# Loading most of x in 32-column strips for VectorE to transpose, and regrouping one expert's rows later, in a routed feed-forward kernel

## The chip, the core and the metric

The kernel runs on one core of one Trainium2 chip. The metric is the device time of one execution in microseconds (us), the median of the runs. The core has five engines with one instruction stream each: TensorE (PE in the profile; PEld is its weight load), VectorE (DVE), ScalarE (ACT), GpSimd (POOL) and SyncE (SP), which here only starts DMAs. Each stream runs in order, so an instruction that waits holds up everything behind it on its engine.

## The reference

x has 4 batches of 1024 tokens of 512 floats. Each batch picks one weight matrix and one bias by its category; a router then sends each token to one of 8 experts, each of which takes at most 512 tokens (4096/8) in token order, and each expert is a two-layer network.

```python
xc   = einsum('bsd,bdh->bsh', x, W[cat]) + b[cat]      # per batch, 512 x 512
p    = softmax(xc @ Wr); e = argmax(p); p_tok = p[e]    # 8 experts
slot = rank of the token among those of its expert      # kept if below 512
h    = relu(xc[dispatch] @ W1[e])                       # 512 -> 2048
y    = (h @ W2[e]) * p_tok                              # 2048 -> 512
out  = x;  out[token] += y                              # for the kept tokens
```

## The kernel before, in words

**Matrix products.** All large products are done by a seven-product scheme (Strassen's, in Winograd's form): operands are cut into quadrants, VectorE makes sums and differences of quadrants (`sums`, `differences`, L163 to L173), TensorE makes seven products k = 1 to 7 in place of eight, and the results are gathered in three accumulators in PSUM called x, y and z (the table `BANK`). VectorE and ScalarE take intermediate states of these accumulators out (the *evictions*), so the next product of the same accumulator waits for them.

**The linear stage** handles x in eight chunks of 512 tokens, chunks 2b and 2b+1 being batch b. `load_x` (L249 to L258) brings a chunk of 1 MB into one of three buffers (the pool `xin`), one token to a row of 2 KB. `transpose_x` is called four times for a chunk; each call turns 128 tokens with four TensorE transposes into PSUM (L276), and ScalarE copies the result to `xT` (L277). After the fourth call VectorE makes the four sums (L293 to L296). `linear` (L491) makes the seven products, `finish` evicts them (L505, L532, L536) and stores the result to two DRAM tensors `xc_dram` (L514). `transpose_w`, `through`, `router`, `choose` and `rank` compute the routing beside it; `rank` scatters each token's number to its slot in DRAM (L463). The tables `beside` and `loads` say behind which product each of these calls stands: TensorE's and SyncE's orders are written out by hand. On VectorE, ScalarE and GpSimd a planner chooses the order, with hints: `soon` puts a step early, `behind` and `issue_after` put it after a named instruction.

**The expert stage** runs e = 0 to 7. `gather` (L704, GpSimd) fetches an expert's rows from `xc_dram`, four gathers for each half of the columns; `fetch(e)` issues those of expert e+1 and then the residual rows of e while expert e's first layer runs. Expert 0's rows are transposed on TensorE (L768). The rows of every later expert are first *regrouped*: `regroup(e, a)` has ScalarE copy pieces of 32 partitions so that the 32 x 32 blocks stand where their transposes belong (L747, 16 copies for an expert, from four calls), and then `turn(e)` has VectorE transpose the blocks (L754, four instructions). `first_layer(e, g, k)` (L787) makes product k of column group g (g = 0 to 3); it snapshots accumulator x after k = 1, 6 and 7 with ScalarE (L802), adds on VectorE (L806) and applies relu on ScalarE (L807, L814). After k = 3 VectorE makes the group's sums (L163 to L166). `second_layer(e, k)` (L848) multiplies all four groups, the last group's quarter last; `inner_product` (L901) makes the remaining products by a second level of the scheme. `between` starts the weight loads and, for expert 0, copies x to the output by DRAM-to-DRAM transfers in three pieces.

In the last group of an expert's first layer the four `regroup(e + 1, ...)` calls stand after products 2, 6, 5 and 7, so ScalarE copies the next expert's rows between its snapshots and relus.

Of the kernel before, what the change touches and what calls it, by code (L numbers as in the profile page):

```python
# [8 lines left out]
F32 = mybir.dt.float32  # L9
# [7 lines left out]
P = 128  # L17
# [5 lines left out]
def kernel(  # L23
# [11 lines left out]
    nc = tc.nc  # L35
    B, S, D = x.shape
    NCAT = cond_w.shape[0]
    E, _, F = w1.shape
    T = B * S
    CAP = -(-T // E)  # L40
    KC = D // P
# [3 lines left out]
    CT = XT * P  # L45
    HT = CT // 2
    SC = CAP // P
    HK = KC // 2
# [3 lines left out]
    NG = F // (2 * HB * P)  # L52
    W1G = 3
    NS = E * SC
    V = 32
    VB = P // V
    Q = 32
    ROW = 2
    xf = x.rearrange("b s d -> (b s) d")
# [38 lines left out]
    ident = const.tile([P, P], F32, name="ident")  # L98
# [78 lines left out]
    def load_w1(e, g):  # L177

        t = w1p.tile([P, 7, HK, HB * P], F32, tag="w1", name=f"w1_{e}_{g}")
        for half in range(2):  # L180
            f = half * F // 2 + g * HB * P
            nc.sync.dma_start(
                out=t[:, 2 * half : 2 * half + 2, :, :].rearrange("p a k f -> p (a k) f"),
                in_=w1[e, :, f : f + HB * P].rearrange("(k p) f -> p k f", p=P),
            )
        w1s[e, g] = t
# [5 lines left out]
    with (  # L192
# [11 lines left out]
        cond, xrows, xT, xS, wT, logits, routed = {}, {}, {}, {}, {}, {}, {}  # L204
# [42 lines left out]

        def load_x(c, eng=nc.sync):
            t = xin.tile([P, XT, D], F32, tag="x", name=f"x_{c}")  # L249
            n = 1 if c == 0 else XT  # L250
            for j in range(0, XT, n):
                eng.dma_start(
                    out=t[:, j : j + n, :],
                    in_=xf[c * CT + j * P : c * CT + (j + n) * P, :].rearrange(
                        "(j p) d -> p j d", p=P
                    ),
                )
            xrows[c] = t  # L258

        def behind_this(f):  # L260
            with tc.issue_after(latest[0].ins):
                latest[0] = f()
# [5 lines left out]
        def transpose_x(b, i):  # L268


            c, j = b * 2 + i // XT, i % XT
            if j == 0:
                xT[c] = xtp.tile([P, KC, CT], F32, tag="xT", name=f"xT_{c}")
            ps = ps_t.tile([P, KC, P], F32, tag="t", name=f"ps_xT_{c}_{j}")
            for kc in range(KC):
                nc.tensor.transpose(ps[:, kc, :], xrows[c][:, j, kc * P : (kc + 1) * P], ident)  # L276
            nc.scalar.copy(xT[c][:, :, j * P : (j + 1) * P], ps)  # L277
            if j == XT - 1:
                a11, a12, a21, a22 = (
                    xT[c][:, k * HK : (k + 1) * HK, half * HT : (half + 1) * HT]  # L280
                    for half in range(2)
                    for k in range(2)
                )
                t = xsp.tile([P, 4, HK, HT], F32, tag="xs", name=f"xs_{c}")
                s1, s2, s3, s4 = (t[:, k, :, :] for k in range(4))
                if c == 2 * LATE + 1:

                    late["all"] = xin.tile([P, XT, D], F32, tag="x", name="late")
                if b == LATE:
                    s4 = lambda g: late["all"][:, 2 + g, :].rearrange("p (k n) -> p k n", n=HT)  # L290
                tt = nc.vector.tensor_tensor
                todo = [
                    lambda: tt(s1, a21, a22, ALU.add),  # L293
                    lambda: tt(s2, s1, a11, ALU.subtract),
                    lambda: tt(s3, a11, a21, ALU.subtract),
                    lambda: tt(s4, a12, s2, ALU.subtract),  # L296
                ]
                if c == 0:

                    b11, b12, b21, b22, t1, t2, t3, t4 = later_sums.pop(0)  # L300
                    todo[1:1] = [lambda: tt(t1, b12, b11, ALU.subtract)]
                    todo[3:3] = [lambda: tt(t2, b22, t1, ALU.subtract)]
                    todo[5:5] = [lambda: tt(t3, b22, b12, ALU.subtract)]
                    todo[7:7] = [lambda: tt(t4, b21, t2, ALU.subtract)]
                    rest = todo[4:]
                    latest[0] = todo[0]()
                    for f in todo[1:4]:
                        behind_this(f)
                    later_sums["rest"] = rest
                else:  # L310
                    if b == LATE:
                        late[c % 2] = (a12, s2)
                        todo[3:] = [
                            lambda g=g: tt(s4(g), *late[g], ALU.subtract)
                            for g in range(2)
                            if c % 2 == 1
                        ]
                    for f in todo:
                        f()
                    if late and b == LATE and c % 2 == 1:  # L320
                        for g in range(2):
                            xS.setdefault((LATE, g), s4(g))
                xS[c] = {1: a11, 2: a12, 3: s4, 4: a22, 5: s1, 6: s2, 7: s3}
# [300 lines left out]
        with tc.manual_schedule(engines={mybir.EngineType.PE, mybir.EngineType.SP}):  # L624
# [3 lines left out]
                out=wr_sb[:, :, 0:E], in_=wr.rearrange("(kc p) e -> p kc e", p=P)  # L628
# [16 lines left out]
            out=table.rearrange("p c e r -> p (c e r)"),  # L645
            in_=slots.rearrange("(p s) r -> p (s r)", p=P),
# [20 lines left out]
    rows, residual, xes, hs = {}, {}, {}, {}  # L667
# [68 lines left out]
    def regroup(e, a):  # L736


        if (e, "strips") not in rows:
            rows[e, "strips"] = xep.tile(  # L740
                [P, KC, SC, VB, V], F32, tag="strips", name=f"strips_{e}"
            )
        r = rows[e, "all"][a * V : (a + 1) * V].rearrange("p s (k b v) -> p s k b v", b=VB, v=V)
        for b in range(VB):
            into = rows[e, "strips"][b * V : (b + 1) * V, :, :, a, :]
            with tc.issue_after(snapped[0].ins):
                nc.scalar.copy(into.rearrange("p k s v -> p s k v"), r[:, :, :, b, :])  # L747
# [231 lines left out]
    with tc.manual_schedule(engines={mybir.EngineType.PE, mybir.EngineType.SP}):  # L979
        gather(0, xg, xc_dram, rows, src_row)  # L980

        for part, half, then in (
            (0, 0, [(0, 1)]),
            (0, 1, [(1, 1), (0, 5), (1, 5)]),
            (1, 0, [(0, 2)]),
            (1, 1, [(1, 2)]),
        ):
            for c in range(half * HC, (half + 1) * HC):
                transpose_rows(0, c, part)
            for g, k in then:  # L990
                first_layer(0, g, k)

        load_w2(0, xes[0][:, 3, 0, HC * P - 1 :])
        for e in range(E):
            for g in range(NG):
                if e == 0 and g < 2:

                    for k in ((6, 7), (4, 3))[g]:
                        first_layer(e, 0, k)
                        first_layer(e, 1, k)  # L1000
                    between(e, g)
                    continue
                first_layer(e, g, 1)
                first_layer(e, g, 2)
                if e + 1 < E and g == NG - 1:
                    regroup(e + 1, 0)
                between(e, g)
                for i, k in enumerate((6, 5, 7)):
                    first_layer(e, g, k)
                    if e + 1 < E and g == NG - 1:  # L1010
                        regroup(e + 1, i + 1)
            second_layer(e, 1)
            first_layer(e, NG - 1, 4)
            inner_sums(e, 2, sides="right")
            first_layer(e, NG - 1, 3)
            inner_sums(e, 2, sides="left")
            if (e + 1) * NG - 1 + W1G < E * NG:
                load_w1(e + 1, W1G - 1)

            def small(*turns):  # L1020
                for k, q in turns:
                    inner_product(e, k, q)

            second_layer(e, 6)
            inner_sums(e, 5)
            small(*[(2, q) for q in (1, 5, 2, 6, 3, 7)])
            second_layer(e, 7)
            small((2, 4))
            inner_sums(e, 3)
            inner_sums(e, 4)  # L1030
            if e + 1 < E:
                turn(e + 1)
            small((5, 5), (5, 2))
            if e + 1 < E:
                sum_xe(e + 1)
            small(
                *[(5, 1), (5, 3), (5, 6), (3, 5), (5, 7), (3, 2), (5, 4), (3, 1)],
                *[(4, 5), (4, 1), (3, 6), (4, 2), (4, 6)],
                *[(3, 3), (4, 3), (3, 7), (4, 7), (3, 4), (4, 4)],
            )  # L1040
            if e + 1 < E:
                load_w2(e + 1)
# [31 lines left out]
```

## Time and profile before

| what | value |
|---|---|
| median of 3 runs (range) | 941.21 us (940.35 to 941.21) |
| the profiled execution's own time | 936.94 us |
| its span, first to last instruction | 935.2 us |
| mean granted TensorE clock | 0.988 of full speed |
| busy share: PE, PEld, DVE, ACT, POOL | 97%, 86%, 71%, 28%, 19% |
| DMA packets, data | 95727, 123.31 MB |
| linear stage | start to about 147 us |
| expert 0 | about 147 to 268 us; experts 1 to 7 about 94 us each |

Times inside the execution are microseconds from the start of its span. In the row of slices each digit stands for a fortieth of the span (23.4 us) and is the busy share in tenths. Matmul durations in the groups overlap, since matmuls are pipelined; the pace of TensorE is read from the distance between starts.

### The profile page before, as it was taken

What the parts mean: (1) busy time and instruction counts of PE and PEld (TensorE: products, weight loads), DVE (VectorE), ACT (ScalarE), POOL (GpSimd) and SP (SyncE); (2) the same over time, 40 slices, a digit from 0 to 9 for tenths busy, and PEclk for the clock granted to TensorE, in tenths of its full rate; (3) what the DMA queues carried; (4) which work ended last, traced back from release to release, by engine and by line L of the source; (5) the groups of instructions that cost most, each with busy time, mean ns of one, the idle gap of its engine ahead of it and who ended that gap; (6) DMA issues with size and microseconds to landing.
All of it is one profiled execution on the core that took longest, in us unless ns stands there. A gap on an engine that the chain in (4) does not pass through costs nothing.

```text
span 935.2 us, 13219 instructions
## 1 busy us (share of the span) xinstructions
PE 902.6 (97%) x5204; PEld 807.9 (86%) x5204; DVE 660.5 (71%) x1226; ACT 264.9 (28%) x506; POOL 176.9 (19%) x173
## 2 busy tenths in 40 slices
PE   9999999928999999999999999999999999999996
PEld 6788787826998899889988998899889988998896
DVE  4656684625946995699569955995599559965893
ACT  3333201305023602360236013601360136013200
POOL 0042343060015001500150015001500140012001
PEclk9999999978999999999999999999999999999999
DMA  9474224991057205620462047214721363136001
GB/s 317 153 233 156 80 92 128 343 372 67 1 177 223 89 8 176 218 84 20 159 220 81 30 154 227 75 42 142 229 81 46 130 221 97 46 119 192 1 1 46
DMA packets 95727, 123.31 MB, mean 132 GB/s; under 512 B 8516, under 2 KB 83268, under 8 KB 95474
## 3 DMA queue, kind: packets, MB, share of 16 engines
q1 hardware_dynamic: 85058, 96.49, 31.3%
q0 software_dynamic: 9216, 24.85, 8.2%
q10 hardware_dynamic: 1392, 1.13, 0.4%
q8 instruction: 41, 0.67, 0.3%
q14 instruction: 20, 0.16, 0.1%
HBM read 105.96 MB, written 25.23 MB: 140 GB/s over the span
## 4 chain that ended last, share of the span: by engine, by line
PE 93%; DVE 2%; DMA 2%; POOL 1%; issue 1%; ACT 0%; POOLq 0%; DVEq 0%
PE hx L787 23%; PE yx L848 18%; PE yx L901 12%; PE hy L787 11%; PE yy L901 6%; PE xcx_lin L491 6%; PE hz L787 5%; PE yz L901 3%; PE xcy_lin L491 2%; PE ps_xT L276 2%; PE xcz_lin L491 1%; DMA rows_of<-xc_dram,at 1%; POOL rows_of L704 1%; PE ps_lT L382 1%; PE ps_wT L330 1%
## 5 line engine op out<-in xcount | busy, mean ns | idle before, releaser
L787 PE MATMUL hx<-xe,w 128*128 128x256 f32 x1024 | 239.6, 382 | 22.5 <-ACT s L802 21.4
L787 PEld LDWEIGHTS hx<-xe,w 128*128 128x128 f32 x1024 | 195.2, 192 | 49.4 <-ACT s L802 21.8
L946 POOL DMA_INDIRECT out_dram<-rows,dst_row x32 | 32.0, 999 | 477.0 <-DVE rows L833 416.4
L787 PE MATMUL hy<-xe,w 128*128 128x256 f32 x512 | 120.6, 379 | 0.0
L848 PE MATMUL yx<-w_b,h 128*128 128x256 f32 x512 | 113.4, 380 | 0.0
L787 PEld LDWEIGHTS hy<-xe,w 128*128 128x128 f32 x512 | 97.5, 190 | 13.0
L848 PEld LDWEIGHTS yx<-w_b,h 128*128 128x128 f32 x512 | 97.3, 191 | 12.8
L802 ACT COPY s<-hx 128x512 f32<-128x512 f32 x96 | 55.8, 581 | 173.0 <-PE hx L787 163.9
L806 DVE TENSOR_TENSOR h<-hy,s 128x512 f32<-128x512 f32 x64 | 44.2, 690 | 78.9 <-PE hy L787 51.6
L807 ACT ACTIVATE h<-h 128x512 f32<-128x512 f32 x96 | 60.5, 630 | 120.3 <-DVE h L806 120.1
L704 POOL DMA_INDIRECT rows_of<-xc_dram,at x56 | 63.1, 1127 | 140.7 <-DVE w L164 94.0
L901 PE MATMUL yx<-w_b,h 128*128 128x128 f32 x640 | 83.2, 275 | 0.0
L901 PEld LDWEIGHTS yx<-w_b,h 128*128 128x128 f32 x640 | 78.5, 192 | 0.8
L747 ACT COPY strips<-rows_of 32x512 f32<-32x512 f32 x112 | 69.0, 616 | 23.6 <-DMA rows<-in_x_dram,at 22.2
L787 PE MATMUL hz<-xe,w 128*128 128x256 f32 x256 | 60.6, 380 | 0.6 <-DVE xe L769 0.6
L806 DVE TENSOR_TENSOR h<-hz,s 128x512 f32<-128x512 f32 x32 | 22.0, 689 | 54.7 <-PE hz L787 54.7
L163 DVE TENSOR_TENSOR h<-h 128x512 f32<-128x512 f32 x64 | 43.7, 683 | 22.1 <-ACT h L807 22.1
L848 PE MATMUL yx<-w_t,h 128*128 128x256 f32 x256 | 56.6, 379 | 0.0
L787 PEld LDWEIGHTS hz<-xe,w 128*128 128x128 f32 x256 | 48.6, 190 | 7.3 <-DVE xe L769 0.9
L848 PEld LDWEIGHTS yx<-w_t,h 128*128 128x128 f32 x256 | 48.7, 190 | 6.5
L463 POOL DMA_INDIRECT slots<-row,dest x32 | 36.3, 1136 | 95.1 <-DVE dest L459 86.6
L901 PE MATMUL yx<-w_t,h 128*128 128x128 f32 x384 | 51.8, 278 | 0.0
(161 smaller groups left out, 1278.6 us busy)
## 6 DMA issues: line engine op xcount, KB each, us to landing
w<-in_L_ffn_W_dram SPq DMA_DIRECT2D x64, 512.0 KB, 4.3
w_b<-in_L_ffn_W_dram SPq DMA_DIRECT2D x32, 1024.0 KB, 10.4
x<-in_x_dram SPq DMA_DIRECT2D x7, 1024.0 KB, 9.3
xc_dram<-s SPq DMA_DIRECT2D x22, 256.0 KB, 2.7
out_dram<-in_x_dram SPq DMA_DIRECT2D x2, 2816.0 KB, 20.6
cw<-in_L_cond_W_dram SPq DMA_DIRECT2D x3, 1024.0 KB, 8.2
out_dram<-in_x_dram SPq DMA_DIRECT2D x1, 2560.0 KB
xc_dram<-xc SPq DMA_DIRECT2D x8, 256.0 KB, 2.3
```

The lines of the kernel that those rows point to most:

```text
L163: eng.tensor_tensor(s1, a21, a22, ALU.add)
L463: nc.gpsimd.indirect_dma_start(out=slots, out_offset=bass.IndirectOffsetOnAxis(ap=dest[:, j : j + 1], axis=0), in_=row[:, j, :], in_offset ...
L491: nc.tensor.matmul(ps[:, j, :], lhsT=left[:, kc, j * P : (j + 1) * P], rhs=right[k][:, kc, :], start=((k in OPENS or (b, k) == (LATE, 3)) ...
L704: nc.gpsimd.indirect_dma_start(out=into[e * SC + c][:, j * n : (j + 1) * n], out_offset=None, in_=source, in_offset=bass.IndirectOffsetOnA ...
L747: nc.scalar.copy(into.rearrange("p k s v -> p s k v"), r[:, :, :, b, :])
L787: nc.tensor.matmul(ps[:, j, :], lhsT=w1s[e, g][:, LEFT[k], kc, j * P : (j + 1) * P], rhs=xes[e][:, RIGHT1[k], kc, :], start=(k in OPENS an ...
L802: snapped[0] = nc.scalar.copy(banks[key, k], ps)
L806: latest[0] = nc.vector.tensor_tensor(into, ps, part, ALU.add)
L807: nc.scalar.activation(into, into, AF.Relu)
L848: nc.tensor.matmul(ps[:, at, :], lhsT=hs[e][:, m // HB, LEFT[k], m % HB, at * P : (at + 1) * P], rhs=w2s[e][RIGHT2[k]][:, m, :], start=(k ...
L901: nc.tensor.matmul(ps, lhsT=left[:, g, :], rhs=right[:, g, :], start=(q in OPENS and g == 0), stop=(q == LAST[BANK[q]] and g == NG - 1), s ...
L946: nc.gpsimd.indirect_dma_start(out=of, out_offset=bass.IndirectOffsetOnAxis(ap=dst_row[:, n : n + 1], axis=0), in_=residual.pop(n), in_off ...
```

## The change

1. `load_x` loads chunks 2 to 7 in another layout. Four transfers replace one. Transfer b fills partitions 32b to 32b+31; its pieces are the columns k·128 + 32b to k·128 + 32b + 31 (k = 0 to 3) of the tokens m·32 + p (m = 0 to 15), each piece 32 floats, 128 bytes. So partition 32b + p holds, for each k and m, 32 columns of one token, and transposing each 32 x 32 block in place gives x transposed.
2. `transpose_x` for chunks 2 to 7: each of its four calls is one VectorE transpose of 128 x 512 elements from the loaded tile to `xT`. The four TensorE transposes into PSUM and the ScalarE copy of such a call are gone. Chunks 0 and 1 stay as they were.
3. The four `regroup(1, ...)` calls no longer stand in the last group of expert 0's first layer. They follow products 4 and 3 of that group and the left inner sums, beside the second layer. For the later experts nothing moves.

```diff
         def load_x(c, eng=nc.sync):
             t = xin.tile([P, XT, D], F32, tag="x", name=f"x_{c}")
+            xrows[c] = t
+            if c > 1:
+                for b in range(VB):
+                    into = t[b * V : (b + 1) * V, :, :].rearrange(
+                        "p k (m v) -> p k m v", v=V
+                    )
+                    rows = xf[c * CT : (c + 1) * CT, :].rearrange(
+                        "(m p) (k b v) -> p b k m v", p=V, b=VB, v=V
+                    )
+                    eng.dma_start(out=into, in_=rows[:, b])
+                return
             n = 1 if c == 0 else XT
...
-            ps = ps_t.tile([P, KC, P], F32, tag="t", name=f"ps_xT_{c}_{j}")
-            for kc in range(KC):
-                nc.tensor.transpose(ps[:, kc, :], xrows[c][:, j, kc * P : (kc + 1) * P], ident)
-            nc.scalar.copy(xT[c][:, :, j * P : (j + 1) * P], ps)
+            if c > 1:
+                half, k = divmod(j, 2)
+                blocks = slice(k * HK, (k + 1) * HK), slice(half * HT, (half + 1) * HT)
+                nc.vector.transpose(xT[c][:, *blocks], xrows[c][:, *blocks])
+            else:
+                ps = ps_t.tile([P, KC, P], F32, tag="t", name=f"ps_xT_{c}_{j}")
+                for kc in range(KC):
+                    nc.tensor.transpose(
+                        ps[:, kc, :], xrows[c][:, j, kc * P : (kc + 1) * P], ident
+                    )
+                nc.scalar.copy(xT[c][:, :, j * P : (j + 1) * P], ps)
...
                 first_layer(e, g, 2)
-                if e + 1 < E and g == NG - 1:
-                    regroup(e + 1, 0)
+                ahead = range(0 if 0 < e < E - 1 and g == NG - 1 else VB, VB)
+                for a in ahead[:1]:
+                    regroup(e + 1, a)
                 between(e, g)
                 for i, k in enumerate((6, 5, 7)):
                     first_layer(e, g, k)
-                    if e + 1 < E and g == NG - 1:
-                        regroup(e + 1, i + 1)
+                    for a in ahead[i + 1 : i + 2]:
+                        regroup(e + 1, a)
             second_layer(e, 1)
             first_layer(e, NG - 1, 4)
             inner_sums(e, 2, sides="right")
...
                 load_w1(e + 1, W1G - 1)
+            if e == 0:
+                for a in range(VB):
+                    regroup(1, a)
```

More of the change, by code (lines that the diff above doesn't have):

```diff
@@ L257, in load_x @@
                 )
-            xrows[c] = t
         def behind_this(f):
```

## The prediction

> **What bounds the kernel now.** First the page: its engine totals, slices and queues.
>
> ```profile
> PE 902.6 (97%) x5204; PEld 807.9 (86%) x5204; DVE 660.5 (71%) x1226; ACT 264.9 (28%) x506; POOL 176.9 (19%) x173
> PE   9999999928999999999999999999999999999996
> PEclk9999999978999999999999999999999999999999
> DMA  9474224991057205620462047214721363136001
> ```
>
> TensorE is the bound everywhere but in slices 9 and 10 (187 to 234 us), where it idles and its clock drops, just after the DMA engines were full. So a gain must shorten TensorE's work or that hole. Next the waits, longest first:
>
> ```profile
> PEld hx L787 <- ACT s L802: 21.8, 1, 21.8
> PE hx L787 <- ACT s L802: 21.4, 1, 21.4
> ACT strips L747 <- DMA rows<-in_x_dram,at: 22.2, 1, 22.2
> ```
>
> One wait holds the 21.4 us. The chain between 180 and 240 us says how: TensorE lacked a snapshot, which stood on ScalarE behind four regroup copies, which waited for GpSimd's gather of expert 1, in flight together with weights and the copy of x to the output.
>
> ```profile
> 196.11 10.92 DMA rows_of<-xc_dram,at
> 207.03 4.24 DMA rows<-in_x_dram,at
> 211.27 0.60 ACT strips L747
> ...
> 214.41 0.48 ACT s L802
> 214.89 0.04 issue
> 214.93 3.78 PE hx L787 x8
> 218.71 7.17 PE yx L848 x32
> 225.88 1.73 PE hx L787 x8
> 227.61 1.73 PE hy L787 x8
> 229.33 6.91 PE yx L848 x32
> ```
>
> For the linear stage, the busy times by stretch (us; then PE, PEld, DVE, ACT, POOL busy with counts; clock, DMA share, GB/s):
>
> ```profile
> 20.00:145.00 125.00, 124.42 (x731) 101.56 (x730) 82.23 (x199) 29.11 (x53) 40.91 (x38) 1.00 0.47 151
> ```
>
> TensorE is full; VectorE is at 66%, the DMA engines at 47%.
>
> **Part 1, what TensorE loses.** In the chain of this stage a group of four x transposes takes one step of length 0.43 to 0.44 us:
>
> ```profile
> 70.93 0.44 PE ps_xT L276 x4
> 71.37 1.73 PE xcx_lin L491 x8
> ```
>
> Six chunks of four groups are 24 x 0.435 = 10.4 us off the bound. (The group's 0.287 us mean times 96 would be 27.6 us, but those durations overlap.) The 24 ScalarE copies removed (0.586 us each) lay beside TensorE: nothing.
>
> **Part 1, what VectorE gets.** The same instruction form stands in the trace: the four transposes of `turn`, 128x512, 694 ns each (28 of them, 18.9 us with overlap). 24 x 0.694 = 16.7 us onto 82.2 in 125 us; after the saving that is 98.9 of 115 us, 86%. It fits, but the queue is in order. In the changed program's VectorE order the four transposes of chunk 4 stand together, 2.8 us, ahead of an eviction (L505), and chunks 3, 5, 6 and 7 have two or three in a row. Behind an eviction waits the accumulator's next product; the product between them covers 1.73 us. So up to 2.8 - 1.7 = 1.1 us a chunk, 6.6 us in all, shows; at the low end the idle gaps (1.2 to 1.7 us before many evictions) take it and it is 0. I take the middle, 3.5 us. Net of part 1 if the loads come in time: -10.4 + 3.5 = about -7.
>
> **Part 1, the loads.** SyncE issues 24 transfers instead of 6: 18 more at the roughly 0.4 us that one x issue takes (row "x SPq": 382 to 1966 ns) are 7 us on a queue that mostly waits. Queued behind them on SP are the stores of xc, the last `load_batch` and expert 0's weights; the weights are due only at 147 us. The price is in the packets: a chunk was 512 packets of 2 KB, and becomes 4 x 32 x 64 = 8192 packets of 128 bytes. No row shows 128 bytes. The DMA view of two stretches with 4-byte packets (the transposed bias) bounds it:
>
> ```profile
> DMA packets 554, 0.48 MB, mean 368 GB/s; under 512 B 321, under 2 KB 321, under 8 KB 554
> q1 hardware_dynamic: 554, 0.48, 108.0%
> ```
>
> That is 21.4 to 22.7 us: 1.08 x 16 x 1.3 = 22.5 us of engine time. Its 233 large packets cost 84 ns each (between 18.5 and 20 us, 299 packets took 100.6% of 24 us), 19.6 us; the 321 small ones share 2.9 us, 9 ns each. Between 9 and 84 ns a straight line gives 13.6 ns at 128 bytes: 8192 x 13.6 / 16 = 7.0 us a chunk, against 512 x 84 / 16 = 2.7 us now. The other end is a stretch in which the small packets went alone:
>
> ```profile
> DMA packets 490, 0.19 MB, mean 127 GB/s; under 512 B 385, under 2 KB 410, under 8 KB 490
> q1 hardware_dynamic: 490, 0.19, 55.8%
> ```
>
> That is 9 to 10.5 us: 3.1 ns a packet over all engines, though they were busy for 56%: 8192 x 3.1 = 25 us a chunk. The gap between the ends is the main unknown.
>
> [...] I take 7 to 9 us, the stretch with a filled queue, as the queue here is filled: x of chunk 2, cw 2, x of chunk 3 are issued back to back.
>
> Is that in time? The load of chunk 2 reaches the engines at about 17 us (the bias packets ahead of it pass at 15.5 to 17 us). At 8 us a chunk, with cw 2 and its bias (about 4 us) behind chunk 2: chunk 2 is there at 25 us and needed at 38 (VectorE's new order puts its transposes behind the scan of batch 0, which ends at 38.3); chunk 3 at 37, needed at about 48; chunk 4 at 47 with stores, needed at 60; chunk 5, whose buffer is free at about 42, at 57, needed at 68; chunk 6 behind cw 3 at 69, needed at 83; chunk 7 at about 82, needed at 90. (The needs are the starts of the old transposes, 31.5 to 106.3 us, less TensorE's saving until then.) All in time: cost 0; extra engine time 6 x 5.3 = 32 us on 59 of 125 us busy, also in. If this cover fails, chunk 7 is late first, and VectorE stands still at its transposes with all evictions behind them.
>
> **Part 2, the regroup.** In the changed program's ScalarE order the last snapshot of group 3 comes first, then two regroup copies, the relu of product 7, thirteen copies, the relu of product 4, one copy, the relu of product 3. GpSimd and the DMAs are untouched, so the rows land at 211.3 on the old axis. TensorE no longer stops at 193.6: product 7 (1.73), `second_layer(0, 1)` (6.91), products 4 and 3 (3.45), then three quarters of `second_layer(0, 6)` (24/32 x 6.91 = 5.2) run to 210.8. The last quarter needs group 3's sums. ScalarE: 211.3 + 16 x 0.62 + 3 relus of 0.6 = 223.0. VectorE has two or three `turn` transposes and two sums (0.65 each) to go: 225.6. So the wait moves: 15 us instead of 21.4. The eight matmuls left run at the low clock as the eight after the old hole did (3.78 us instead of 1.73): say 3.5, end 229.1. Before, `second_layer(0, 6)` ended at 229.33 + 6.91 = 236.24. Gain 7.1 us; 9 at most with no clock loss, 4 if the inner sums behind it are late.
>
> **Sum.** 936.94 (own time of the profiled execution) - 7 - 7 = 923. The median of the runs is 4.27 us above that execution; 923 + 4.3 = 927.
>
> **Rivals.**
> *Small packets set the pace (slower).* Place: the x queue. For: 25 us a chunk in the lonely stretch. Against: the filled stretches. Chunk 7 comes at 17 + 6r + about 17 us of other traffic and is needed at 90, so nothing shows up to r = 9 us; 14 us of gain are eaten at r = 12 (23 ns a packet on each engine), from where the kernel is slower; at r = 15, 941 + 20 = about 960; at 25, chunk 7 is there at 184, 94 late: about 1020.
> *VectorE binds.* All 16.7 us show: -10.4 + 16.7 - 7.1 = -0.8, about 940: no change. For: 86% and an in-order queue. Against: its idle gaps.
> *The regroup gains nothing*, because the rows land later still or the sums behind them slip: 927 + 7 = 934.
>
> **How the numbers follow.** Likeliest, both parts as worked out: 0.48, 927, own range 918 to 935 (part 1 between -10.4 and -4, part 2 between -9 and -4). Regroup without gain: 0.10. VectorE binds: 0.10, half of it within 0.2% (1.9 us, what a measurement here can tell), the rest split. Small packets: 0.32, of it 0.27 above 943. With the tails: faster 0.61, same 0.06, slower 0.33. The range 916 to 978 leaves out under 0.05 below and about 0.15 (r over 17) above.
>
> **What the profile after would show.** Right: the x transfers' packets under 512 B rise by some 49,000; the stage up to the first L787 row ends near 140 us; the VectorE transposes of the linear stage wait for nothing; the wait of L787 for the snapshot is gone and one of about 15 us stands before the second layer. Wrong: VectorE's transposes waiting for "DMA x" in the waits, or a DMA row near 9 from 17 to 120 us (packets); TensorE waiting for L505 and L532 with the DMAs idle (VectorE).

## The result, and the profile after

The changed kernel takes 950.61 us, median of six runs (946.22 to 952.38), beside 941.15 for the kernel before (940.35 to 942.04): ratio 1.0091, 95% interval 1.0074 to 1.0107. It is slower by about 9 us, where 14 us of gain were forecast. The profiled execution took 947.42 us, its span is 945.6 us.

The page after: engine totals, three rows of the slices, and the packets.

```profile
PE 901.7 (95%) x5108; PEld 799.7 (85%) x5108; DVE 674.5 (71%) x1250; ACT 250.7 (27%) x482; POOL 176.9 (19%) x173
...
PE   9978799994999999999999999999999999999996
...
PEclk9999999997899999999999999999999999999999
DMA  8997314795047214721362137213731373136001
...
DMA packets 142094, 123.29 MB, mean 130 GB/s; under 512 B 57956, under 2 KB 132708, under 8 KB 141842
```

The new holes are in slices 3 to 5 (47 to 118 us), inside the linear stage, where TensorE was full before. In this row the granted clock falls below 0.9 only in slices 10 and 11, at the hole of expert 0. The same stretch as in the prediction, 20 to 145 us:

```profile
20.00:145.00 125.00, 108.23 (x584) 83.56 (x583) 91.34 (x216) 15.44 (x29) 35.02 (x32) 0.97 0.62 144
```

TensorE did 584 matmuls in it and idled for 17 us, at a mean clock of 0.97, although VectorE was busy for only 91 of 125 us and the DMA engines for 62%. No engine was full. TensorE's timeline names who was late (only rows with idle time before them are shown; the bracket holds that idle time and what ended it):

```profile
42.61 1.64 PE L402 MATMUL ps_lT<-xT,wrc 128*32 128x512 f32 x8 [1.47 <-DVE xT L290]
52.01 1.56 PE L402 MATMUL ps_lT<-xT,wrc 128*32 128x512 f32 x8 [1.49 <-DVE xT L290]
65.70 3.42 PE L511 MATMUL xcx_lin<-wd,xs 128*128 128x256 f32 x8 [4.61 <-DVE s L525]
83.92 1.99 PE L511 MATMUL xcx_lin<-wd,xs 128*128 128x256 f32 x8 [2.86 <-DVE s L525]
101.08 1.99 PE L511 MATMUL xcx_lin<-wd,xs 128*128 128x256 f32 x8 [2.76 <-DVE s L525]
116.45 3.65 PE L511 MATMUL xcx_lin<-wd,xs 128*128 128x256 f32 x8 [3.16 <-DVE s L525]
```

Four times the accumulator x could take no further product until VectorE had taken its state out (L525, the L505 of before), and twice the router waited for a turned x. After two of the four long waits eight matmuls took nearly twice as long (3.42 and 3.65 us at a granted clock of 0.57 and 0.54, where such a group takes 1.89 to 1.99); after the other two the clock was 1.00. VectorE ahead of the first long wait, in the timeline:

```profile
59.64 0.29 DVE L391 TENSOR_REDUCE lg<-ps_l 128x32 f32<-128x128 f32 x1 [3.00 <-PE ps_wT L350]
59.97 0.22 DVE L426 TENSOR_REDUCE top<-lg 128x8 f32<-128x64 f32 x1
...
62.40 0.17 DVE L445 COPY scan<-carry 128x8 f32<-128x8 f32 x1
62.58 2.49 DVE L290 STREAM_TRANSPOSE xT<-x 128x512 f32<-128x512 f32 x4
64.99 0.65 DVE L525 TENSOR_TENSOR s<-xcx_lin,cb 128x512 f32<-128x512 f32 x1
```

The eviction at 64.99 had its input at about 58.05 (the eight matmuls started at 56.16 and take 1.89). In the queue ahead of it stood a reduction that waited 3.0 us for logits (1.6 us of it after 58.05), that reduction with the choice of experts (2.9 us), and all four turns of chunk 4 (2.49 us). No turn waited for a load. In the kernel before, the same eviction stood ahead of that reduction and of the choice:

```profile
57.59 0.69 DVE L505 TENSOR_TENSOR s<-xcx_lin,cb 128x512 f32<-128x512 f32 x1 [1.47 <-PE xcx_lin L491]
58.20 0.28 DVE L371 TENSOR_REDUCE lg<-ps_l 128x32 f32<-128x128 f32 x1
```

So not only the turns were new in VectorE's queue: other instructions had changed places too.

The first hx row of expert 0, which ends the linear stage, moves from 147.52 to 158.55 us: 11.0 us later, although 10.4 us of transposes have left TensorE. So the stage lost 21.4 us. In the second part, the time from the first hx of expert 0 to that of expert 1 falls from 120.6 to 115.3 us. The 21.4 us wait on the snapshot is gone and two others stand in TensorE's timeline:

```profile
225.08 7.40 PE L868 MATMUL yx<-w_t,h 128*128 128x256 f32 x24 [8.39 <-DVE rows L853]
237.47 3.78 PE L868 MATMUL yx<-w_t,h 128*128 128x256 f32 x8 [4.99 <-DVE h L164]
```

Experts 1 to 6 take 95.0 us each in this trace and 94.2 in the trace before, 4.8 us together. That does not come with the change: with the same expert stage the intervals are 94.2 us in two kernels below, as the last section tells. 11.0 - 5.3 + 4.8 = 10.5 us, the 10.4 between the spans.

### The profile page after: what moved, and what is told of

Its sections match the earlier page's. It is cut to its first block, busy times and chain, and to the rows that moved or that the text cites. A ratio compares the mean times of both kernels' runs of the same rounds, so it can differ in the third digit from the quotient of the medians.

```text
span 945.6 us, 13044 instructions
## 1 busy us (share of the span) xinstructions
PE 901.7 (95%) x5108; PEld 799.7 (85%) x5108; DVE 674.5 (71%) x1250; ACT 250.7 (27%) x482; POOL 176.9 (19%) x173
## 3 DMA queue, kind: packets, MB, share of 16 engines
q1 hardware_dynamic: 131426, 96.49, 33.2%
## 4 chain that ended last, share of the span: by engine, by line
PE 89%; DVE 5%; POOL 1%; issue 1%; ACT 1%; DMA 1%; POOLq 0%; DVEq 0%; ACTq 0%
PE hx L807 22%; PE yx L868 16%; PE yx L921 12%; PE hy L807 11%; PE xcx_lin L511 6%; PE yy L921 6%; PE hz L807 5%; PE yz L921 3%; PE xcy_lin L511 2%; POOL rows_of L724 1%; DMA rows_of<-xc_dram,at 1%; PE xcz_lin L511 1%; ACT strips L767 1%; DVE xT L290 1%; PE ps_lT L402 1%
## 5 line engine op out<-in xcount | busy, mean ns | idle before, releaser
L807 PE MATMUL hy<-xe,w 128*128 128x256 f32 x512 | 120.6, 379 | 0.0
L868 PE MATMUL yx<-w_t,h 128*128 128x256 f32 x256 | 60.7, 397 | 13.4 <-DVE rows L853 8.4
L868 PEld LDWEIGHTS yx<-w_t,h 128*128 128x128 f32 x256 | 50.9, 200 | 21.6 <-DVE rows L853 8.8
L853 DVE SCALAR_TENSOR_TENSOR rows<-yx,table,rows 128x256 f32<-128x256 f32 (+1 forms) x88 | 34.9, 440 | 16.9 <-DMA rows<-in_x_dram,at 10.5
```

Source lines behind the costliest of these rows:

```text
L807: nc.tensor.matmul(ps[:, j, :], lhsT=w1s[e, g][:, LEFT[k], kc, j * P : (j + 1) * P], rhs=xes[e][:, RIGHT1[k], kc, :], start=(k in OPENS an ...
L853: nc.vector.scalar_tensor_tensor(row, ps, table[:, half * HC + at, e, 0:1], row, ALU.mult, ALU.add)
L868: nc.tensor.matmul(ps[:, at, :], lhsT=hs[e][:, m // HB, LEFT[k], m % HB, at * P : (at + 1) * P], rhs=w2s[e][RIGHT2[k]][:, m, :], start=(k ...
```

## The experiments

Times of the stage below are the start of the first hx row. Each ratio is to the kernel before, timed beside it on the same chip; since that kernel took 936.5 to 940.9 us there and 941.15 in the first runs, the times that were expected are compared by their ratio. The theory at the start was that VectorE, not the packets, costs the stage.

**The parts apart.** Four kernels: each part alone, and each half of part 1 alone, the halves with the regroup of before. In a half alone the load and the turn no longer fit together, so its result is another one, with the same number and sizes of operations.

```diff
 # the second part alone: load_x and transpose_x as before, regroup calls as changed
 # the first part alone: load_x and transpose_x as changed, regroup calls as before
 # strip loads, turned by TensorE (c > NT is never true: NT is 32, c at most 7)
 def transpose_x(b, i):
...
-            if c > 1:
+            if c > NT:
 # row loads, turned by VectorE
 def load_x(c, eng=nc.sync):
...
-            if c > 1:
+            if c > NT:
```

The first part alone:

> The first part of the change alone: strips loaded and turned by VectorE, expert 1's rows regrouped where the kernel before does it. If the loss of the linear stage comes from VectorE (theory): the first hx row of expert 0 at about 158.5 us as in the changed kernel, against 147.5 before; the 21.4 us wait of the second expert's start stays; about 951 to 957 us, the upper end if the 0.8 us that each of experts 1 to 6 lost comes from this part as well. Rival, the second part cost something that the first hides: 945 or less.

Measured: 947.81 us, ratio 1.0126 (1.0108 to 1.0143), first hx at 157.33, the snapshot wait still 21.2 us. The loss is in this part. On the scale of the first runs the ratio is 953 us. The experts took 94.22 us each, so the 0.8 us an expert is no part of this loss.

The second part alone:

> The second part alone, x loaded and turned as before. Theory: the first hx at 147.5 us, expert 0 to expert 1 in 115.4 us in place of 120.8 (the wait on the residual rows, 8.4 us, and the one on the strips, 5.0 us, take the place of the 21.4), so 936 us; 941 if the 0.8 us an expert goes with this part. Rival (the whole 15 us wait that the prediction had): 934 us.

Measured: 930.18 us, ratio 0.9936 (0.9920 to 0.9953). First hx at 147.52, expert 0 to expert 1 in 113.47 us. It gains 6.7 us in time and 7.1 in the trace, where 5.2 to 5.4 were expected here; by its ratio it stands at 935 us. The waits are of the kind expected, 6.9 us for the residual rows and 5.3 for the strips.

Strip loads, turn left to TensorE:

> The 32-column strip loads of chunks 2 to 7 with the turn left on TensorE and ScalarE, regroup as before. x of chunks 2 to 7 is then not in the order that the turn assumes, so other data is routed; the number and sizes of all operations are those of before. Theory (VectorE's order, not the packets, costs the stage): first hx within 2 us of 147.5, 941 us within 2. Rival, the small packets or SP's blocking at their issue set the pace: first hx at 152 us or later, 946 us or more.

Measured: 943.75 us, ratio 1.0067 (1.0042 to 1.0093), first hx at 153.51, not within 2 us of 147.5. The theory fell here: 6.0 us lost without one turn on VectorE.

Row loads, turned by VectorE:

> Chunks 2 to 7 loaded by rows as before, in large packets, but turned by VectorE's 32 x 32 block transposes, regroup as before; x of these chunks is then transposed inside its 32 x 32 blocks alone, so other data is routed. Theory (VectorE): first hx at 156 to 159 us, 950 to 957 us. Rival (small packets): the TensorE saving comes through, first hx at 137 to 142 us, 931 to 937 us.

Measured: 928.60 us, ratio 0.9920 (0.9902 to 0.9938), first hx at 137.74. It fell here too: VectorE does the same 24 turns and the stage is 9.8 us shorter, nearly all of the 10.4. But the rival (packets) doesn't fit either, since no turn in the changed kernel waits for a load.

**What the two misses had in common.** Set side by side, the programs of the first part alone and of "row loads, turned by VectorE" have the same order on TensorE, ScalarE and GpSimd; SyncE's differs in the loads alone. VectorE's order differs in 73 lines. The planner orders VectorE's queue, and it does so differently when only the shape of a load changes. With row loads it puts the turns of chunks 2 to 4 very early; with strips it puts them late and in heaps. "Strip loads, turned by TensorE" differs from the kernel before in VectorE's order as well, although it has no turn there. So each of the two had changed two things. The new theory: the order, not the amount and not the packets, costs most of the stage's loss. To test it the order was written by hand, as edges of issue order from each VectorE instruction of the stage to the next:

```diff
+dve = [i for i in nc.cur_bb.bb.instructions if i.engine == mybir.EngineType.DVE]
+order = [int(n) for n in ORDER_DVE.split()]     # an order of the stage's instructions
...
+for a, b in zip(order, order[1:]):
+    tc.add_manual_dep(
+        dve[b],
+        dve[a].name,
+        mybir.DependencyInfo(mybir.DependencyClass.NoSync, mybir.DependencyReason.DATA),
+        reason="order",
+    )
```

Strips with VectorE's order of the row loads:

> Strips loaded and turned by VectorE, regroup as before, and VectorE's queue in the stage put by hand in the order that the compiler gave it with row loads (73 lines of the order differ from the run with the strips alone; TensorE's order is the same). Theory, order: the compiler takes the strip loads for slow and so puts the turns behind the choice of experts, in one heap ahead of the sums that TensorE waits for, and with the other order the loss goes: first hx of expert 0 at 138 to 142 us, ratio to the kernel before 0.990 to 0.997. Rival, arrival: the strips themselves come late on the chip, VectorE waits for them, first hx at 150 us or later, ratio 1.005 or more.

Measured: 944.17 us, ratio 1.0073 (1.0054 to 1.0092), first hx at 154.09. The rival holds for this order: its first turns stand ahead of their strips. VectorE's timeline:

```profile
24.54 2.49 DVE L305 STREAM_TRANSPOSE xT<-x 128x512 f32<-128x512 f32 x4 [8.37 <-DMA x<-in_x_dram]
...
35.52 1.30 DVE L305 STREAM_TRANSPOSE xT<-x 128x512 f32<-128x512 f32 x2 [4.71 <-DMA x<-in_x_dram]
...
42.47 1.90 DVE L305 STREAM_TRANSPOSE xT<-x 128x512 f32<-128x512 f32 x3 [3.09 <-DMA x<-in_x_dram]
```

VectorE stands still 21.4 us in five such waits, with the evictions behind it. (In the kernels with a written order, the next one aside, ScalarE's order moved too: in two places an exponential of the choice and a copy beside it changed order. What that alone does was not tried.) The rows also give the landing of chunks 2, 3 and 4: 24.5, 35.5 and 42.5 us.

Row loads with VectorE's order of the strips:

> The reverse: row loads in large packets, turned by VectorE (x of chunks 2 to 7 is transposed inside its 32 x 32 blocks alone), with VectorE's queue in the order of the run with the strips alone. Theory, order: first hx at 152 to 158 us, ratio 1.006 to 1.013 although no small packet is moved. Rival, arrival: first hx at 137 to 141 us, ratio 0.990 to 0.995.

Measured: 947.02 us (944.75 to 953.05), ratio 1.0130 (1.0096 to 1.0164), first hx at 155.32. The theory holds: chunks 2 to 7 come in large packets, VectorE's order is the only one that differs from the kernel that gave 137.74, and the stage is nearly as slow as with strips. TensorE's timeline has the same four waits:

```profile
64.03 1.99 PE L525 MATMUL xcx_lin<-wd,xs 128*128 128x256 f32 x8 [3.38 <-DVE s L539]
80.82 1.99 PE L525 MATMUL xcx_lin<-wd,xs 128*128 128x256 f32 x8 [2.85 <-DVE s L539]
97.87 1.99 PE L525 MATMUL xcx_lin<-wd,xs 128*128 128x256 f32 x8 [2.65 <-DVE s L539]
113.24 3.42 PE L525 MATMUL xcx_lin<-wd,xs 128*128 128x256 f32 x8 [3.16 <-DVE s L539]
```

The changed kernel whole, with the order of the row loads:

> The changed kernel whole, with VectorE's queue in the stage in the order that row loads give. Theory, order, with the second part's gain added: first hx at 138 to 142 us, expert 0 to expert 1 in 113.5 to 115.5 us, ratio 0.983 to 0.990; up to 5 us more if experts 1 to 6 keep the 0.8 us each that they lost in the changed kernel. Rival, arrival: first hx at 150 us or later, ratio 0.998 or more.

Measured: 937.74 us, ratio 1.0012 (1.0003 to 1.0022), first hx at 155.29, expert 0 to expert 1 in 113.68 us, experts at 94.21. The stage went as with strips and that order before, and the second part's gain came on top: 1.0073 to 1.0012.

Strip loads turned by TensorE, with VectorE's order of the kernel before:

> Strip loads turned by TensorE as in the run with the strip loads alone (x of chunks 2 to 7 in another order, so other data is routed), with VectorE's queue in the order of the kernel before. Theory, order: most of the 6.0 us that the strip loads alone cost goes, first hx at 148 to 150 us, ratio 1.000 to 1.003. Rival, arrival: first hx at 153 us again, ratio 1.006 or more.

Measured: 937.86 us, ratio 1.0011 (1.0002 to 1.0021), first hx at 147.41. The whole 6.0 us goes with the order. The stretch of the stage, as in the prediction:

```profile
20.00:145.00 125.00, 124.41 (x731) 101.38 (x730) 81.94 (x199) 28.86 (x52) 40.92 (x38) 1.00 0.68 159
```

TensorE is as full as before (124.42), with most of the strips' 49,152 packets of 128 bytes (8192 a chunk) beside it. They raise the DMA share from 0.47 to 0.68 and cost nothing in the stage (first hx at 147.52 before). The first hx (us) in the combinations that were run:

| turned by, VectorE's order | row loads | strip loads |
|---|---|---|
| TensorE, order of the kernel before | 147.5 | 147.4 |
| TensorE, order planned for strips | not run | 153.5 |
| VectorE, order planned for rows | 137.7 | 154.1 |
| VectorE, order planned for strips | 155.3 | 157.3 |

Each order has its own cost: the one planned for rows is too early for strips (16.4 us), the one planned for strips costs 17.6 us with row loads and puts the turns late and in heaps. How much of the 17.6 us is the heaps, and how much the other instructions that the planner moved, no run separates; that the others can cost too is shown by the 6.0 us lost with no turn on VectorE. A good order has to keep clear of all of this.

**An order clear of both.** VectorE's order of the kernel before, and each of the 24 turns put in where ScalarE had copied that turn's result when TensorE did it, with times from the trace of the kernel just shown. The second part is as in the change.

> The changed kernel whole, with VectorE's queue in the stage in the order of the kernel before, and each of the 24 turns put in where ScalarE copied that turn from PSUM when TensorE did it (in the trace of strip loads with the queue of before, where nothing waited for the strips). Theory, two bounds on the place of a turn (not ahead of its strips, not in one heap ahead of the sums TensorE waits for): neither wait comes, first hx at 138 to 143 us, expert 0 to expert 1 in 113.5 to 115.5, ratio 0.983 to 0.990. Rival, VectorE's amount of work is too much for the stage with strips in any order: first hx at 147 us or later, ratio 0.994 or more.

Measured: 931.23 us, ratio 0.9896 (0.9879 to 0.9912), first hx at 143.84, expert 0 to expert 1 in 115.28. It beats the kernel before, but the stage ended just over the range, with 4.7 us of waits for VectorE left on TensorE in it, 0.8 of them for a turn.

The same, each turn 1.5 us earlier:

> As the run with the turns spread, each turn 1.5 us earlier in VectorE's queue. What it tells: on which side of the place of a turn the rest of the stage's loss lies (first hx at 143.8 us there, 137.7 with row loads). Theory, the turns were a little late: first hx at 140 to 143 us, ratio 0.984 to 0.989. Rival, the strips are only just there: VectorE waits for them, first hx at 146 us or later, ratio 0.992 or more. Beside it: whether 95.0 us from expert to expert, or 94.2, goes with it.

Measured: 922.52 us (921.94 to 922.91), ratio 0.9850 (0.9834 to 0.9866), first hx at 138.94, earlier than the 140 to 143 expected; the waits for VectorE are down to 2.2 us. This is the changed kernel with nothing altered but the order of VectorE's queue in one stage (and the two places on ScalarE), and it is 14.3 us faster than the kernel before and the fastest of all that were run. The other instructions on VectorE are back in the order of the kernel before, so the gain over the changed kernel, 19.6 us in the stage (158.55 to 138.94), is that of both together. VectorE around the place of the heap, in its timeline:

```profile
56.47 0.22 DVE L449 TENSOR_REDUCE best<-won 128x8 f32<-128x64 f32 x1
56.64 0.71 DVE L305 STREAM_TRANSPOSE xT<-x 128x512 f32<-128x512 f32 x1
58.55 0.22 DVE L473 TENSOR_REDUCE total<-ex 128x8 f32<-128x64 f32 x1 [1.19 <-ACT ex L471]
...
60.12 0.69 DVE L540 TENSOR_TENSOR s<-xcx_lin,cb 128x512 f32<-128x512 f32 x1
...
61.52 0.70 DVE L305 STREAM_TRANSPOSE xT<-x 128x512 f32<-128x512 f32 x1
62.46 0.69 DVE L540 TENSOR_TENSOR s<-xcx_lin,cb 128x512 f32<-128x512 f32 x1 [0.23 <-PE xcx_lin L526]
...
63.73 0.70 DVE L305 STREAM_TRANSPOSE xT<-x 128x512 f32<-128x512 f32 x1
...
64.63 0.69 DVE L540 TENSOR_TENSOR xc<-xcx_lin,cb 128x512 f32<-128x512 f32 x1 [0.15 <-PE xcx_lin L526]
...
65.44 0.70 DVE L305 STREAM_TRANSPOSE xT<-x 128x512 f32<-128x512 f32 x1
```

One turn at a time, with an eviction between. The busy times of its stage:

```profile
20.00:138.00 118.00, 115.67 (x643) 92.17 (x641) 95.36 (x224) 15.23 (x29) 38.97 (x38) 1.00 0.73 171
```

VectorE is at 81%, TensorE at 98%, and no turn waits for a load.

**The copies of x to the output earlier.** On the kernel with the turns spread, a try at the waits that are left in expert 0:

```diff
 def between(e, g):
-        if e == 0 and g > 0:
-            q = slice((g - 1) * T // (NG - 1) // P * P, g * T // (NG - 1) // P * P)
-            nc.sync.dma_start(out=of[q, :], in_=xf[q, :])
...
 loads = {
...
+            (2, 6): [(copy_out, 1)],
+            (2, 10): [(copy_out, 2)],
+            (3, 1): [(copy_out, 3)],
```

> As the one with the turns spread, and the three copies of x into the output (8 MB from DRAM to DRAM, issued between the first-layer groups of expert 0 before) issued in the stage's third and fourth batch instead, where the DMA engines are 22 to 59% busy. Theory: the residual rows and expert 1's rows wait for their packets behind these copies (DMA share 1.0 from 170 to 220 us), so both of expert 0's remaining waits (7.8 and 4.3 us in the run with the row order) go: expert 0 to expert 1 in 101 to 106 us, ratio 0.968 to 0.979. Rival, the gathers are slow by themselves or the copies hold up the last gather before expert 0: 113 us or more, or the gain lost ahead of the first hx.

Measured: 934.00 us, ratio 0.9924 (0.9907 to 0.9940): slower by 2.8 us than without. Expert 0 to expert 1 took 111.77 us, 3.5 less, but the first hx came at 149.73, 5.9 later: TensorE waited 4.8 us for expert 0's gathered rows. These were issued late: GpSimd waited 11.38 us for the table of slots, beside 2.87 without the move, and the first gather began at 142.81 in place of 135.73. In expert 0 one wait shrank and one stayed:

```profile
217.88 8.38 PE L901 MATMUL yx<-w_t,h 128*128 128x256 f32 x24 [7.14 <-DVE rows L886]
226.47 1.99 PE L901 MATMUL yx<-w_t,h 128*128 128x256 f32 x8 [0.22 <-DVE h L179]
```

So the wait on the strips goes with the copies (3.94 us without the move), and the wait on the residual rows for the most part does not (9.28). What makes the residual rows late stays open.

**The changed kernel once more.**

> The changed kernel once more, beside the runs below. What it is asked: whether the 0.81 us that each of experts 1 to 6 lost in its first trace belongs to the program (then 95.0 us from expert to expert again) or to that execution (then 94.22, and a ratio near 1.004). First hx at 157 to 159 us in both cases.

Measured: 947.56 us beside 940.89, ratio 1.0080 (1.0058 to 1.0102), first hx at 158.78, experts at 95.0 us again (one at 94.4). The loss is there again; the last section tells of the 95.0 us.

## Why the prediction was wrong

*TensorE's saving, 10.4 us.* Right: with row loads and their order the stage is 9.8 us shorter, in the best strip kernel 8.6.

*VectorE's queue, 0 to 6.6 us, taken as 3.5.* This step failed. In its place stand 21.4 us in the changed kernel, about 2 of them from the strips themselves. VectorE's order alone costs 17.6 us with row loads, and 19.6 us lie between the changed kernel's order and the best one with strips. (17.6 for the order, 2.0 for the strips, 0.6 of the saving that did not come with row loads either, and 1.2 us between the first part alone and the changed kernel, which stay unexplained, make the 21.4.) The heaps were seen: the prediction named the four turns of chunk 4 ahead of an eviction. It priced a heap as its own length less the 1.73 us product beside it, 1.1 us. But what an eviction waits for is everything in the queue ahead of it, from the moment its input is there: 1.6 us in which a reduction still waited for logits, 2.9 us of that reduction and the choice, and 2.49 us of turns. So the eviction came 7 us late; 3.0 us of other TensorE work covered part, and 4.6 showed. That the choice stood ahead of this eviction was itself new: the prediction looked for the turns in the new order, not for what else had moved. Before the eviction at the second long wait stood sums and weight differences in a row and then three turns. The slow matmuls after a hole (3.42 and 3.65 us at a granted clock of 0.57 and 0.54), which the prediction counted in the second part, were left out here. "It fits, but the queue is in order" was the right sentence; the total of 86% (81% in the best kernel) was never the limit, so the rival *VectorE binds* has the right engine and the wrong reason. Its worst case, 16.7 us, was all of the turns' own time, and the loss exceeded it.

*The loads: in time at 7 to 9 us a chunk, cost 0.* Right, and close where a row shows the landing: chunk 2 was expected at 25 us and came at 24.5, chunk 3 at 37 (35.5), chunk 4 at 47 (42.5). The extra engine time is (0.68 - 0.47) x 125 = 26 us for six chunks, 4.4 a chunk on the 2.7 of before, so 7.1 us against the 7.0 worked out (6.6 by the q1 shares in the last section). SyncE's part was mis-sized: four issues of strips held it 5.4 to 11.6 us in the changed kernel, 45 us for the six chunks, where 0.4 us an issue was taken. It cost the stage nothing: first hx at 147.41 with the strips and the order of before. The needs were worked out from the old places of the transposes, and that is why the order planned for rows, which moved the turns ahead of those places, waited. The rival *small packets set the pace*, which held most of the chance of slower, was the wrong reason for the right sign: in the changed kernel's order the strips add 2.0 us (155.32 to 157.33).

*The regroup, 7.1 us.* Right in size: 7.1 alone in the trace, 5.3 and 6.9 in the two traces of the changed kernel. Wrong in its make-up: one wait of 15 us before the last quarter of `second_layer(0, 6)` was forecast. There were two. The first, 6.9 to 9.3 us in these runs, stands before its first product: the accumulator is still held by `second_layer(0, 1)`, whose addition into the residual rows (L853) waits for these rows. VectorE's timeline in the changed kernel:

```profile
223.81 0.48 DVE L853 SCALAR_TENSOR_TENSOR rows<-yx,table,rows 128x256 f32<-128x256 f32 x1 [10.28 <-DMA rows<-in_x_dram,at]
```

The wait was there to be read in the trace of before, in GpSimd's order: the residual rows are gathered after expert 1's. The second is the forecast one, shorter because the first took part of its time; in the second part alone it ended at 224.96 us, where 225.6 was forecast. So the size could hold although a wait was overlooked. Together they are 12 to 14 us.

*The sum, 923 on the profiled execution's axis.* The kernel with the turns 1.5 us earlier comes to it: 922.42 in its profiled execution, with 8.6 us from the stage (7 forecast) and 6.0 from expert 0 (7.1 forecast). The forecast took such an order for the one that the program had.

What the prediction said the profile would show: packets under 512 B rose by 49,440 (some 49,000 forecast), turns wait for no load, and the snapshot wait is gone. The stage did not end near 140 us but at 158.55. "TensorE waiting for L505 and L532 with the DMAs idle (VectorE)" is the sign of the wrong case that came, with the DMA engines idle in part alone: their share was 0.98, 0.85, 0.03 and 0.27 in the four long waits.

## What to carry to other kernels

On an engine whose queue is in order, price added work by where each piece stands: for every instruction that the bounding engine waits for, add up all that is queued ahead of it from the moment its input is ready, waits included; for one eviction that was 7 us here. Where a planner orders the queue, a change to a load can reorder arithmetic that it doesn't touch; compare the orders before believing that two kernels differ only in the edit, and pin the order when the load itself is to be measured. The turns moved to another engine went best spread out, a little ahead of where their old result was copied (first hx at 138.94 us): not ahead of their data (154.09 in that order), not in heaps (157.33 in that one).

## What the runs showed of the hardware

Packets of 128 bytes raised the DMA engines' time without costing TensorE any: in the order of before it was busy for 124.41 of the 125 us from 20 to 145 us with strip loads, and for 124.42 in the kernel before. The row of q1 before, and with strip loads turned by TensorE in the order of before:

```profile
q1 hardware_dynamic: 85058, 96.49, 31.3%
q1 hardware_dynamic: 131426, 96.49, 33.8%
```

The same 96.49 MB in 46,400 more packets took 2.5% more of the 16 engines' span, 23.5 us or 3.9 us for each of six chunks.

The issue of a chunk's four transfers, 2048 packets of 128 bytes each, held SyncE for 5.4 to 11.6 us in the changed kernel, and that of the one transfer of large packets for 0.4 to 2.0 us in the kernel before. One group of four from SyncE's timeline in the changed kernel, and the issue of the same chunk in the kernel before:

```profile
24.46 8.56 SPq L261 DMA_DIRECT2D x<-in_x_dram  x4
16.28 1.18 SPq L252 DMA_DIRECT2D x<-in_x_dram  x1
```

The time from expert to expert is 94.2 or 95.0 us for the same instructions. It was 95.0 in both traces of the changed kernel, with the turns spread, and with the copies early; 94.2 in the others (three kernels have one interval of 94.4 to 94.5), the changed kernel with the row order and the one with the turns earlier among them, whose expert stage has the same order of instructions on every engine. In the changed kernel's first trace the waits have it so, once an expert:

```profile
ACT s L822 <- remote: 11.7, 6, 2.0
...
PE hx L807 <- issue: 3.2, 6, 0.6
```

(The numbers are the sum in us, how often, and the longest; "remote" stands for a releaser that the profile cannot name.)

Once an expert a snapshot on ScalarE starts 1.6 us later after the instruction ahead of it than in the kernel before, and with it the work behind it, and TensorE waits 0.5 us with nothing named. The second trace of the changed kernel and the other two 95.0 us kernels ran on one chip; there the kernel before took 940.89 us, against 936.54 to 936.83 on the three other chips of the experiments. So the kernel before may have it too on that chip (6 x 0.81 = 4.9 us, the difference is 4.1 to 4.4), and the 4.27 us between the median of before and its profiled execution may be the same thing; neither was traced. What causes it stays open.
